# Other steps for the last layer's edges, scale, shift and final norms in a four-layer graph kernel

## The chip, the cores and the metric

The kernel runs on one core of one Trainium2 chip. The metric is the device time of one execution in microseconds; lower is better. Before the change, three runs gave 3883.53 to 3885.66 us, median 3884.97 us.

## The reference

There are 16 batches of 1024 nodes with 128 features, and one adjacency matrix for all. Three graph attention layers (8 heads of 16) come first, then one last layer of another kind. In short:

```python
# layers 0, 1, 2
scores = einsum('bnhd,bmhd->bhnm', h @ Wq, h @ Wk) / 4
attn = softmax(where(adj == 0, -inf, scores))
x = layer_norm(h + (attn @ (h @ Wv)) @ Wo + bo) * ln1_g + ln1_b
x = layer_norm(x + relu(x @ W1 + b1) @ W2 + b2) * ln2_g + ln2_b
# last layer
h = x @ W
e = leaky_relu((h @ a_src)[:, :, None] + (h @ a_dst)[:, None, :], 0.2)
att = softmax(where(adj == 0, -inf, e))
out = ln_gamma * layer_norm(att @ h + x) + ln_beta
```

Everything is in 32-bit floating point.

## The kernel before

**Blocks and steps.** A block is one batch through one of the three attention layers. There are 48 blocks, in passes of four batches: layer 0 of batches 0 to 3, layer 1 of the same four, layer 2 of the same four, then the next four batches (L848). A block has 32 steps: two head groups `g`, two halves of the queries `qh`, eight key tiles `kt`. Below, 11:29 means step 29 of block 11, counted from 0. In one step TensorE (PE) makes four score matmuls (L546). One half of the scores goes to ScalarE (ACT) for the exponential (L554) and then to GpSimd (POOL), which multiplies by the 0/1 mask (L555). The other half gets an additive mask on VectorE (DVE, L558) and then its exponential on ScalarE (L570). In ten of the 32 steps, listed in `BOTH_ON_DVE`, both halves take the second way and POOL has no product. The attention matmuls of a step (L575) run four steps later (`AHEAD`), into one PSUM accumulator.

**Other work between the steps.** All other work is cut into small tasks. `put` appends a chain of tasks, each with a gap in steps after the one before it and with flags. `piece` is called once per step. It takes at most one task that issues PE work per step; tasks with `*` in their flags come free beside it. A chain with a table (`AT`) has its tasks at fixed steps. `POOL_FREE` names the only steps at which tasks with `~` or `^` may be taken. `need` forces the tasks up to a mark at once; `need(source(m + 1))` does so at the head of a block, for the input of the next one.

- `proj_tasks` (L458) makes the queries and keys of the next block. Each half is split in a high part (ScalarE, L473) and a low part (VectorE, L474 or L478), and the copies in `stack` (L531) put them in place, 16 transfers at step 24 and 16 at step 1.
- `post_tasks` (L595) is the rest of a layer: output projection, norm, FFN, norm. `normalise` (L425) runs on POOL: negate the mean (L434), add epsilon (L435), power -0.5 (L436), subtract and scale per tile (L442). Its residual scale and shift (L633) are two POOL operations at steps 22 and 24.
- `last_tasks` (L702) is the last layer of one batch. It transposes x (L346), makes the node values (`nodes`, L721), sends eight rows twice as small copies to `g_rows` and `h_rows` (`send_rows`, L753, 16 transfers), and then, for each of eight tiles v, makes the edges (eight matmuls L773, and four masked maxima on VectorE, L778) and aggregates them two turns later (64 PE matmuls L384, then L798, L799 and the statistics on VectorE). Two POOL operations named `scaled` (L717, L718, both through L811) multiply x by ln2_g and add ln2_b; aggregates need their result. After four tiles `norm` normalises the lower half, after eight the upper; two POOL operations each (L811) apply gamma and beta, and `store` writes a half out in four transfers.

The last layers of a pass lie in the blocks of the next pass: batch 0's begins in block 10, batch 3's ends in block 16. Blocks 22 to 28 and 34 to 40 repeat this. The last pass's lies in blocks 46 and 47 and in a tail after the last step.

**What sets the order.** On PE, ScalarE and SyncE (SP) instructions stand in the order of the program. On VectorE and POOL a scheduler orders them by priority; `tc.issue_after` keeps an instruction behind another on its engine. `behind["pool"]` is the latest mask product, `low[n]` is the low part made at step n. One PSUM bank `t` serves all tasks, so a task's matmuls wait until the task before has been read out. SP issues nearly all transfers, in order; a transfer that waits holds back those behind it. There are five buffers for x, so the fetch of a later batch waits until the stores of an earlier one have landed.

Of the kernel before, what the change touches and what calls it, by code (L numbers as in the profile page):

```python
# [15 lines left out]
OP = mybir.AluOpType  # L16
AX = mybir.AxisListType

P = 128
# [4 lines left out]
SLOT = 32  # L24
# [5 lines left out]
LANES = 4  # L30
# [7 lines left out]
STACK_AT = 24  # L38
AT_END = {3: (12, 21, 22, 24, 25, 26, 27, 28, 30, 31), 2: (8, 9, 13, 14, 15, 16, 17, 18, 20, 21)}
AHEAD = 4  # L40
POOL_FREE = {"~": (0, 1, 2, 3, 4, 5, 6, 22, 23), "^": (30, 31, 0, 1, 2, 3, 4, 5, 6)}
BOTH_ON_DVE = (3, 7, 8, 15, 23, 24, 26, 28, 30, 31)
TILES = {"w": 8, "x": LANES + 1, "last": 2}
BLOCKED = -57344.0
# [76 lines left out]
def fast_path(ctx: ExitStack, tc: tile.TileContext, a: dict, out: bass.AP, flag):  # L121
    nc = tc.nc
    x_dram, adj = a["x"], a["adj"]
    B, N, D = x_dram.shape
    NT = N // P
# [14 lines left out]
    def bank():  # L140

        if head[0] or tail[0]:
            return slot()[:, :512]
        return psum.tile([P, 512], F32, tag="t", name="t", bufs=1)
# [14 lines left out]
    def tokens(v):  # L159

        return v.rearrange("(h j t e) d -> j e h t d", h=2, j=4, t=4)
# [33 lines left out]
    mask01 = const.tile([P, NT, N], F8W)  # L195
# [51 lines left out]
    wl = {}  # L247
# [177 lines left out]
    def normalise(n, ts):  # L425

        scalars(n, ts)
        subtract_scale(n, ts)

    def scalars(n, ts):  # L430

        mv = n[2]
        m, v = mv[:, ts, 0], mv[:, ts, 1]
        nc.gpsimd.tensor_scalar(m, m, -1.0, None, op0=OP.mult)  # L434
        nc.gpsimd.tensor_scalar(v, v, EPS, None, op0=OP.add)  # L435
        nc.gpsimd.tensor_tensor(v, v, half_neg[:, ts], OP.pow)  # L436

    def subtract_scale(n, ts):

        z, _, mv = n  # L440
        for t in range(ts.start, ts.stop):
            nc.gpsimd.tensor_scalar(z[:, t, :], z[:, t, :], mv[:, t, 0:1], mv[:, t, 1:2], op0=OP.add, op1=OP.mult)  # L442
# [79 lines left out]
    behind, low = {}, {}  # L522
# [179 lines left out]
    def last_tasks(b):  # L702
        s = {}
# [17 lines left out]
        def nodes(t0, t1):  # L721
            def run():
                col, ts = s["col"], slice(t0, t1)

                halves = [slice(max(t0, 4 * h), min(t1, 4 * h + 4)) for h in range(2)]
                halves = [(c, s["hd"][c.start // 4][:, c.start % 4:(c.stop - 1) % 4 + 1, :])
                          for c in halves if c.start < c.stop]
                ps = bank()
                for t in range(t0, t1):
                    by_columns(ps[:, (t - t0) * (D + 2):(t - t0 + 1) * (D + 2)],  # L730
                               s["xT", t // 4][:, t % 4 * P:(t % 4 + 1) * P], w_nodes)
                pv = ps[:, :(t1 - t0) * (D + 2)].rearrange("p (t d) -> p t d", d=D + 2)
                with soon():
                    nc.scalar.activation(col[:, 2, ts], pv[:, :, D + 1], AF.Exp, scale=NEG_SLOPE)
                    nc.scalar.activation(col[:, 0:2, ts].rearrange("p c t -> p t c"), pv[:, :, D:], AF.Exp,
                                         scale=1 - NEG_SLOPE)
                    for c, hd in halves:
                        nc.vector.tensor_mul(hd[:, :, :D], pv[:, c.start - t0:c.stop - t0, :D],
                                             col[:, 2, c, None].to_broadcast([P, c.stop - c.start, D]))
                for c, hd in halves:  # L740
                    nc.scalar.copy(hd[:, :, D], col[:, 2, c])
            return run
# [22 lines left out]
        def edges(v):  # L765
            def run():
                e = s["e", v] = edge_tile().rearrange("p (k q) -> p k q", q=P)
                half, t = slice(v // 4 * 512, v // 4 * 512 + 512), v % 4 * SLOT
                ps = slot()
                for k in range(4):  # L770
                    for r in range(2):
                        row = slice(64 * r + g0, 64 * r + g0 + 4)
                        nc.tensor.matmul(ps[:, r * 512 + k * P:r * 512 + (k + 1) * P], h_rows[row, k * P:(k + 1) * P],  # L773
                                         g_rows[row, half].rearrange("p (j q) -> p j q", j=4)[:, :, t:t + SLOT],
                                         start=True, stop=True)
                for j in range(4):
                    q = v // 4 * 512 + j * P + t
                    nc.vector.scalar_tensor_tensor(e[:, :, j * SLOT:(j + 1) * SLOT],  # L778
                                                   ps.rearrange("p (k q) -> p k q", q=P)[:, :, j * SLOT:(j + 1) * SLOT],
                                                   1.0, mask01[:, :, q:q + SLOT], op0=OP.max, op1=OP.mult)  # L780
            return run

        mul, add = nc.gpsimd.tensor_mul, nc.gpsimd.tensor_add
        late = b % LANES == LANES - 1 and b < B - 1

        def norm(h):
            def run():
                with tc.issue_after(behind["pool"]):
                    normalise(s["n"], slice(4 * h, 4 * h + 4))
            return run  # L790

        def aggregate(v):
            def run():
                need_if(("scaled", b))
                e, ps = s["e", v], bank()
                for t in range(NT):
                    by_columns(ps[:, :D + 1], e[:, t, :], s["hd"][t // 4][:, t % 4, :], start=(t == 0), stop=(t == NT - 1))
                nc.vector.reciprocal(s["col"][:, 3, v:v + 1], ps[:, D:D + 1])  # L798
                nc.vector.scalar_tensor_tensor(s["n"][0][:, v, :], ps[:, :D], s["col"][:, 3, v:v + 1],  # L799
                                               state["x", b][:, v, :], op0=OP.mult, op1=OP.add)  # L800
                stats(s["n"], slice(v, v + 1))
                if v % 4 == 3 and (v < NT - 1 or not late):
                    norm(v // 4)()
                if v == NT - 1:
                    check_range(s["col"].rearrange("p c t -> p (c t)"))
            return run

        def by_rows(op, z, v, n=NT):
            def run():
                with tc.issue_after(behind["pool"]):  # L810
                    op(z(), z(), rows(v(), n))  # L811
            return run
# [1 line left out]
        def x():  # L814
            return state["x", b]

        def y(h):
            return lambda: s["n"][0][:, 4 * h:4 * h + 4, :]

        def store(h):  # L820
            def run():
                y = s["n"][0]
                queue = nc.scalar if h and b == B - 1 else nc.sync
                for j in range(4):
                    queue.dma_start(tokens(out[b])[j][:, h], y[j * SLOT:(j + 1) * SLOT, 4 * h:4 * h + 4, :])

            return run

        def two(f, g):
            def run():  # L830
# [2 lines left out]
            return run  # L833

        tasks = [(5, xt(0), "+w +last +w +w"), (1, xt(1), "+w"), (2, nodes(0, 3), ""), (2, nodes(3, 6), ""),
                 (2, nodes(6, 8), "-w -w"), (2, rows_gh, ""), (1, send_rows, "*"), (7 if b < B - 1 else 4, edges(0), "")]
        for v in range(NT - 1):
            tasks.append((2, two(edges(v + 1), aggregate(v)), ""))
            if v in (4, 6):
                tasks.append((0, by_rows((mul, add)[v // 2 - 2], y(0), lambda v=v: wl[("ln_gamma", "ln_beta")[v // 2 - 2]], 4), "*"))  # L840
        up = "*^" if late else "*"
        tasks += [(2, aggregate(NT - 1), ""), (2, store(0), "-last -w -w *")] + [(0, norm(1), up)] * late
        tasks += [(1, by_rows(mul, y(1), lambda: wl["ln_gamma"], 4), up), (2 - late, by_rows(add, y(1), lambda: wl["ln_beta"], 4), up),
                  (3, store(1), "-x *")]
        return tasks


# [3 lines left out]
    now = [0]  # L851
# [3 lines left out]
    def put(tasks, mark, chain=None, first=False, table=None):  # L855

        if chain is None:
            chain = {"due": now[0], "queue": deque()}
            chains.insert(0 if first else len(chains), chain)
        for n, task in enumerate(tasks):  # L860
            at = now[0] // (4 * NT) * 4 * NT + (table or AT[mark[0]])[n] if mark[0] in AT else None
            chain["queue"].append(task + (mark if n == len(tasks) - 1 else None, at))
        return chain
# [16 lines left out]
    def is_due(chain):  # L880
        gap, tiles, at = chain["queue"][0][0], chain["queue"][0][2], chain["queue"][0][4]
        if now[0] >= 4 * NT * len(blocks):
            gap -= gap == 2
        for c in POOL_FREE:
            if c in tiles and not tail[0] and now[0] % (4 * NT) not in POOL_FREE[c]:
                return False
# [21 lines left out]
    with tc.manual_schedule(engines={mybir.EngineType.PE, mybir.EngineType.Activation, mybir.EngineType.DVE,  # L908
# [9 lines left out]
        ps = {}  # L918
# [55 lines left out]
    n = 0  # L974
    with tc.manual_schedule(engines={mybir.EngineType.PE, mybir.EngineType.Activation, mybir.EngineType.SP}):
        for m, (b, l) in enumerate(blocks):
# [3 lines left out]
            for at, (g, qh, kt) in enumerate((g, qh, kt) for g, qh in order for kt in range(NT)):  # L980
# [5 lines left out]
                if m + 1 < len(blocks):  # L986
# [5 lines left out]
                    if at == (6 if m == 0 else 0):  # L992
                        late = any(c["queue"][-1][3] == ("xP", m + 1) for c in chains)
# [6 lines left out]
                if FIRST <= n < FIRST + 4:  # L1000

                    with tc.manual_schedule(engines={mybir.EngineType.DVE}):
                        e = score_step(step)
                        neighbours(4 + n - FIRST)
                        masks(4 + n - FIRST, mask_rows(4 + n - FIRST))
                else:
                    e = score_step(step)
# [26 lines left out]
    ps = bank()  # L1034
# [226 lines left out]
```

## Time and profile before

| what | value |
|---|---|
| median of three runs | 3884.97 us |
| the profiled execution | 3886.72 us |
| its span, first to last instruction | 3884.9 us |
| PE busy | 3710.5 us (96%) |
| VectorE busy | 3460.0 us (89%) |
| POOL busy | 3477.8 us (90%) |
| ScalarE busy | 3295.4 us (85%) |
| mean granted PE clock | 0.987 |
| additive masks, L558 | 2016 of 1212 ns |
| mask products on POOL, L555 | 1056 of 2029 ns |
| edge maxima, L778 | 512 of 415 ns |
| pow on POOL, L436 | 179 of 1196 ns |
| subtract and scale on POOL, L442 | 896 of 448 ns |

The profile is one execution. All times within it are counted from the first instruction. Busy time of an engine includes no waiting; "idle before" names the wait just ahead of an instruction and the instruction or transfer that ended it. The granted clock is the share of TensorE's full speed that the hardware allowed in a stretch. The first score matmul of block 10 starts at 745.0 us, of block 11 at 817.7, 12 at 918.0, 13 at 1012.9, 14 at 1103.1, 15 at 1189.0. The last block's first is at 3669.2 and the tail begins at about 3770.

### The profile page before, as it was taken

To read this page: it belongs to the slowest core of one execution; us is meant where nothing else is said; L and a number is where in the kernel's file an instruction comes from. 1 tells how busy PE (TensorE), PEld (TensorE's weight loads), DVE (VectorE), ACT (ScalarE), POOL (GpSimd) and SP (SyncE) were. 2 spreads that over 40 slices of the span, in tenths; PEclk is the share of its full clock that TensorE was granted. 3 is DMA by queue.
4 is the path that set the end of the run, shared out by engine and by line. 5 is a ranking of instruction groups with operands and counts; after the bars stand their busy time and mean duration, and the time that the engine had idled before them with its cause. 6 is when DMAs were issued, how large, how long until landed. Compare 5 with 4: busy or idle time off the path is not lost.

```text
span 3884.9 us, 109698 instructions
## 1 busy us (share of the span) xinstructions
PE 3710.5 (96%) x44385; PEld 1513.9 (39%) x44385; DVE 3460.0 (89%) x5860; ACT 3295.4 (85%) x3797; POOL 3477.8 (90%) x2971
## 2 busy tenths in 40 slices
PE   7999999999999999999999999999999999999998
PEld 2333333344444333334444433333444433333346
DVE  6999999988989899998898999999889998999876
ACT  7989999977888999997788899999677799999860
POOL 4899999988988999998888999999788899999885
PEclk8999999999999999999999999999999999999998
DMA  5434324322233324332233324324222323423200
GB/s 138 114 74 101 96 72 107 90 67 67 73 79 84 103 69 104 91 80 74 67 85 79 93 67 101 96 72 101 70 70 63 96 72 90 107 69 104 71 5 24
DMA packets 245887, 319.28 MB, mean 82 GB/s; under 512 B 51072, under 2 KB 174208, under 8 KB 245376
## 3 DMA queue, kind: packets, MB, share of 16 engines
q1 hardware_dynamic: 243840, 311.52, 31.5%
q8 instruction: 353, 5.78, 0.6%
q14 instruction: 158, 1.29, 0.1%
q10 hardware_dynamic: 1536, 0.68, 0.1%
HBM read 58.53 MB, written 51.38 MB: 28 GB/s over the span
## 4 chain that ended last, share of the span: by engine, by line
POOL 45%; PE 38%; ACT 7%; DVE 5%; issue 3%; SPq 1%; DMA 1%; DVEq 0%; ACTq 0%; POOLq 0%
POOL e L555 27%; PE acc L575 13%; PE t L384 12%; PE s L546 9%; POOL x L442 6%; POOL x L633 4%; POOL mv L436 4%; ACT e L554 3%; ACT e L570 3%; DVE e L558 3%; PE s L773 2%; POOL x L811 1%; PE s L384 1%; POOL A L590 1%; POOL mv L435 1%
## 5 line engine op out<-in xcount | busy, mean ns | idle before, releaser
L558 DVE TENSOR_TENSOR e<-s,mask_add 128x1024 f32<-128x1024 f32 x2016 | 2377.8, 1212 | 203.7 <-PE s L546 175.5
L555 POOL TENSOR_TENSOR e<-e,mask 128x1024 f32<-128x1024 f32 x1056 | 2120.1, 2029 | 215.3 <-ACT e L554 201.9
L570 ACT ACTIVATE e<-e 128x1024 f32<-128x1024 f32 x2016 | 2109.9, 1062 | 175.9 <-DVE e L558 148.7
L575 PE MATMUL acc<-e,v 128*17 128x512 f32 x12288 | 1625.1, 601 | 70.3 <-POOL e L555 57.0
L554 ACT ACTIVATE e<-s 128x1024 f32<-128x1024 f32 x1056 | 1085.0, 1027 | 264.8 <-PE s L546 260.4
L546 PE MATMUL s<-Wq,Wk 64*128 64x512 f32 x6144 | 1195.1, 458 | 29.6 <-DVE e L558 17.0
L546 PEld LDWEIGHTS s<-Wq,Wk 64*128 64x128 f32 x6144 | 498.7, 185 | 1080.8 <-issue 386.9
L575 PEld LDWEIGHTS acc<-e,v 128*17 128x17 f32 x12288 | 204.7, 95 | 584.3 <-issue 350.2
L442 POOL TENSOR_SCALAR x<-x,mv 128x128 f32<-128x128 f32 x896 | 388.1, 448 | 19.4
L436 POOL TENSOR_TENSOR mv<-mv,half_neg 128x4 f32<-128x4 f32 (+1 forms) x179 | 214.1, 1196 | 14.0
L384 PE MATMUL t<-hd,ee 128*32 128x129 f32 x6720 | 214.9, 280 | 7.0 <-DVE lo L474 6.6
L414 DVE BATCH_NORM_STATS2 st<-x 128x6 f32<-128x128 f32 x896 | 204.4, 282 | 7.7
L384 PE MATMUL t<-x1T,W 128*32 128x512 f32 x1520 | 200.8, 600 | 1.4 <-DVE parts L750 1.3
L778 DVE SCALAR_TENSOR_TENSOR ee<-s,mask 128x256 f32<-128x256 f32 x512 | 180.2, 415 | 24.2 <-PE s L773 20.7
L384 PEld LDWEIGHTS t<-hd,ee 128*32 128x32 f32 x6720 | 187.1, 112 | 22.6 <-issue 11.2
L384 PEld LDWEIGHTS t<-W,hT 128*32 128x32 f32 x6080 | 171.0, 111 | 59.3 <-issue 48.7
L384 PE MATMUL t<-W,hT 128*32 128x128 f32 x6080 | 185.1, 274 | 0.1
L421 DVE TENSOR_TENSOR x<-t,x 128x512 f32<-128x512 f32 x191 | 129.1, 676 | 36.4 <-PE t L384 35.6
L590 POOL TENSOR_TENSOR A<-tt,recs 128x256 f32<-128x256 f32 x192 | 120.0, 625 | 43.5 <-DVE recs L589 43.5
L650 ACT ACTIVATE hT<-t,b 128x512 f32<-128x512 f32 x190 | 130.8, 688 | 13.6 <-PE t L384 12.7
L586 DVE STREAM_TRANSPOSE tt<-acc 128x512 f32<-128x512 f32 x192 | 135.5, 706 | 0.0
L358 DVE STREAM_TRANSPOSE xb<-x 128x512 f32<-128x512 f32 x164 | 115.1, 702 | 10.1 <-POOL x L442 9.8
(145 smaller groups left out, 2515.8 us busy)
## 6 DMA issues: line engine op xcount, KB each, us to landing
Wk<-hi SPq DMA_DIRECT2D x384, 128.0 KB
Wk<-lo SPq DMA_DIRECT2D x384, 128.0 KB
Wq<-hi SPq DMA_DIRECT2D x384, 128.0 KB
Wq<-lo SPq DMA_DIRECT2D x384, 128.0 KB
tr<-xb SPq DMA_DIRECT2D x656, 64.0 KB
x1T<-tr SPq DMA_DIRECT2D x90, 256.0 KB
xT<-tr SPq DMA_DIRECT2D x74, 256.0 KB
x<-in_x_dram SPq DMA_DIRECT2D x124, 64.0 KB
```

The source lines that it names most:

```text
L384: nc.tensor.matmul(dst[j:j + SLOT, :], cols, rhs, start=start, stop=stop)
L414: nc.vector.bn_stats(st[:, t, :], z[:, t, :])
L436: nc.gpsimd.tensor_tensor(v, v, half_neg[:, ts], OP.pow)
L442: nc.gpsimd.tensor_scalar(z[:, t, :], z[:, t, :], mv[:, t, 0:1], mv[:, t, 1:2], op0=OP.add, op1=OP.mult)
L546: nc.tensor.matmul(ps[:, r * 512:(r + 1) * 512], k[64 * r:64 * r + 64, kt * P:(kt + 1) * P], q[64 * r:64 * r + 64, q0:q0 + 512], start=Tru ...
L554: nc.scalar.activation(ev, psv, AF.Exp, scale=HD ** -0.5)
L555: behind["pool"] = nc.gpsimd.tensor_mul(ev, ev, m).ins
L558: behind["dve"] = nc.vector.tensor_add(ev, psv, m).ins
L570: nc.scalar.activation(ev, ev, AF.Exp, scale=HD ** -0.5)
L575: nc.tensor.matmul(acc[j * SLOT:j * SLOT + HD + 1, :], v_bufs[m % 2][:, kt, 2 * j + g, :], e[:, j, :], start=first, stop=last)
L590: nc.gpsimd.tensor_mul(state["A"][:, qh, :, g, :], tt[:, :, :HD], rec[:, :, None].to_broadcast([P, 16, HD]))
L778: nc.vector.scalar_tensor_tensor(e[:, :, j * SLOT:(j + 1) * SLOT], ps.rearrange("p (k q) -> p k q", q=P)[:, :, j * SLOT:(j + 1) * SLOT], 1 ...
```

## The change

There are four edits.

1. In the last layer, the gap before the first edges is 9 turns instead of 7 for every fourth batch (0, 4, 8, 12). For batch 15 it stays 4, for the others 7.
2. The steps at which the `scaled` operations may be taken are 0 to 6, 27, 28 and 29 instead of 0 to 6, 22 and 23.
3. The masked maxima of the edges are issued behind the low part of the step before, where there was one.
4. For batch 15, tiles 4 to 7 are each normalised, scaled, shifted and stored by themselves, as a chain of four tasks put at the head of the list when the tile is aggregated, instead of together after tile 7. The four transfers of such a store go to SP and ScalarE's queue in turns; before, the upper half's four went to ScalarE's queue. `norm`, `y` and `store` take a slice of tiles instead of a half.

```diff
-POOL_FREE = {"~": (0, 1, 2, 3, 4, 5, 6, 22, 23), "^": (30, 31, 0, 1, 2, 3, 4, 5, 6)}
+POOL_FREE = {"~": (0, 1, 2, 3, 4, 5, 6, 27, 28, 29), "^": (30, 31, 0, 1, 2, 3, 4, 5, 6)}
...
-                    nc.vector.scalar_tensor_tensor(e[:, :, j * SLOT:(j + 1) * SLOT],
-                                                   ps.rearrange("p (k q) -> p k q", q=P)[:, :, j * SLOT:(j + 1) * SLOT],
-                                                   1.0, mask01[:, :, q:q + SLOT], op0=OP.max, op1=OP.mult)
+                    with tc.issue_after(low[now[0] - 1]) if now[0] - 1 in low else nullcontext():
+                        nc.vector.scalar_tensor_tensor(e[:, :, j * SLOT:(j + 1) * SLOT],
+                                                       ps.rearrange("p (k q) -> p k q", q=P)[:, :, j * SLOT:(j + 1) * SLOT],
+                                                       1.0, mask01[:, :, q:q + SLOT], op0=OP.max, op1=OP.mult)
...
-                if v % 4 == 3 and (v < NT - 1 or not late):
-                    norm(v // 4)()
+                if b == B - 1 and v > 3:
+                    put([(0, norm(slice(v, v + 1)), "*"), (0, by_rows(mul, y(slice(v, v + 1)), lambda: wl["ln_gamma"], 1), "*"),
+                         (0, by_rows(add, y(slice(v, v + 1)), lambda: wl["ln_beta"], 1), "*"),
+                         (0, store(slice(v, v + 1)), "*")], ("out", v), first=True)
+                elif v % 4 == 3 and (v < NT - 1 or not late):
+                    norm(slice(v - 3, v + 1))()
...
-                queue = nc.scalar if h and b == B - 1 else nc.sync
                 for j in range(4):
-                    queue.dma_start(tokens(out[b])[j][:, h], y[j * SLOT:(j + 1) * SLOT, 4 * h:4 * h + 4, :])
+                    queue = nc.scalar if j % 2 and b == B - 1 and ts.start > 3 else nc.sync
+                    queue.dma_start(tokens(out[b])[j][:, ts.start // 4, ts.start % 4:(ts.stop - 1) % 4 + 1],
+                                    y[j * SLOT:(j + 1) * SLOT, ts, :])
...
-                 (2, nodes(6, 8), "-w -w"), (2, rows_gh, ""), (1, send_rows, "*"), (7 if b < B - 1 else 4, edges(0), "")]
+                 (2, nodes(6, 8), "-w -w"), (2, rows_gh, ""), (1, send_rows, "*"), (4 if b == B - 1 else 9 if b % LANES == 0 else 7, edges(0), "")]
...
-        tasks += [(1, by_rows(mul, y(1), lambda: wl["ln_gamma"], 4), up), (2 - late, by_rows(add, y(1), lambda: wl["ln_beta"], 4), up),
-                  (3, store(1), "-x *")]
+        if b < B - 1:
+            tasks += [(1, by_rows(mul, y(h1), lambda: wl["ln_gamma"], 4), up),
+                      (2 - late, by_rows(add, y(h1), lambda: wl["ln_beta"], 4), up), (3, store(h1), "-x *")]
```

More of the change, by code (lines that the diff above doesn't have):

```diff
@@ L784, in last_tasks, with norm @@
         late = b % LANES == LANES - 1 and b < B - 1
-        def norm(h):
+        def norm(ts):
             def run():
                 with tc.issue_after(behind["pool"]):
-                    normalise(s["n"], slice(4 * h, 4 * h + 4))
+                    normalise(s["n"], ts)
             return run
@@ L815, in x, with y, store @@
             return state["x", b]
-        def y(h):
-            return lambda: s["n"][0][:, 4 * h:4 * h + 4, :]
-        def store(h):
+        def y(ts):
+            return lambda: s["n"][0][:, ts, :]
+        def store(ts):
             def run():
                 y = s["n"][0]
-                queue = nc.scalar if h and b == B - 1 else nc.sync
                 for j in range(4):
-                    queue.dma_start(tokens(out[b])[j][:, h], y[j * SLOT:(j + 1) * SLOT, 4 * h:4 * h + 4, :])
+                    queue = nc.scalar if j % 2 and b == B - 1 and ts.start > 3 else nc.sync
+                    queue.dma_start(tokens(out[b])[j][:, ts.start // 4, ts.start % 4:(ts.stop - 1) % 4 + 1],
+                                    y[j * SLOT:(j + 1) * SLOT, ts, :])
             return run
@@ L839, in last_tasks @@
             if v in (4, 6):
-                tasks.append((0, by_rows((mul, add)[v // 2 - 2], y(0), lambda v=v: wl[("ln_gamma", "ln_beta")[v // 2 - 2]], 4), "*"))
+                tasks.append((0, by_rows((mul, add)[v // 2 - 2], y(slice(0, 4)), lambda v=v: wl[("ln_gamma", "ln_beta")[v // 2 - 2]], 4), "*"))
         up = "*^" if late else "*"
-        tasks += [(2, aggregate(NT - 1), ""), (2, store(0), "-last -w -w *")] + [(0, norm(1), up)] * late
-        tasks += [(1, by_rows(mul, y(1), lambda: wl["ln_gamma"], 4), up), (2 - late, by_rows(add, y(1), lambda: wl["ln_beta"], 4), up),
-                  (3, store(1), "-x *")]
+        h1 = slice(4, NT)
+        tasks += [(2, aggregate(NT - 1), ""), (2, store(slice(0, 4)), "-last -w -w *")] + [(0, norm(h1), up)] * late
+        if b < B - 1:
+            tasks += [(1, by_rows(mul, y(h1), lambda: wl["ln_gamma"], 4), up),
+                      (2 - late, by_rows(add, y(h1), lambda: wl["ln_beta"], 4), up), (3, store(h1), "-x *")]
         return tasks
```

## The prediction

> **What bounds the kernel now.** I read the page first: PE 96% busy, VectorE 89%, ScalarE 85%, POOL 90%. An average over stages says little, so I cut the span at the first score matmul of each block (32 steps of one batch and layer) and asked for busy times by stretch. Columns: stretch, its length, busy time and count of PE, weight loads, VectorE (DVE), ScalarE (ACT), POOL, then the granted PE clock.
>
> ```profile
> 463.00:533.40 70.40, 68.53 (x708) 24.09 (x704) 65.43 (x99) 67.06 (x75) 67.63 (x56) 1.00 0.35 91
> 817.70:918.00 100.30, 93.61 (x1357) 44.69 (x1353) 83.52 (x168) 70.48 (x88) 79.09 (x73) 0.97 0.26 68
> 918.00:1012.90 94.90, 92.16 (x1324) 44.75 (x1320) 82.52 (x164) 69.90 (x82) 79.21 (x73) 0.98 0.28 71
> ```
>
> A plain block (463) is PE at 97%. Blocks 11 and 12, which also carry the last layer of batches 0 and 1, hold 6.7 and 2.7 us of PE idle and a clock below 1. Block 13 has 0.5 us of idle. PE's work is the same after the change, so it can win only idle PE time and lost clock, and lose only by new PE waits. Next, PE's timeline for idle time over 1 us in blocks 10 to 13 (in brackets: idle before, releaser):
>
> ```profile
> 823.32 0.63 PE L773 MATMUL s<-g_rows,h_rows 4*128 4x128 f32 x7 [3.64 <-DMA h_rows<-parts]
> ...
> 909.56 1.91 PE L575 MATMUL acc<-e,v 128*17 128x512 f32 x8 [2.48 <-POOL e L555]
> ...
> 946.85 3.46 PE L384 MATMUL t<-hd,ee 128*32 128x129 f32 x60 [2.21 <-DVE lo L474]
> ```
>
> These are steps 11:0 (block:step), 11:29 and 12:10. The groups of batches 4 and 8 repeat them (3.66, 2.49, 2.21 and 4.68, 2.50, 2.20 us). Each is followed by 3.4 us at half clock:
>
> ```profile
> 909.30:912.70 3.40, 3.14 (x16) 0.55 (x16) 0.00 (x0) 0.13 (x1) 3.40 (x4) 0.51 0.02 5
> 1320.10:1323.50 3.40, 3.14 (x28) 0.76 (x28) 1.87 (x2) 1.70 (x3) 3.40 (x3) 1.00 0.36 92
> ```
>
> The second row follows an idle of 1.80 us and keeps clock 1.00. After 909.56 eight attention matmuls took 1.68 us against 0.87 elsewhere, and eight FFN matmuls 1.72 against 0.97: about 1.6 us lost per drop.
>
> [...] The rows show drops after 2.21 and 2.48 us, so 4.8. [...] I take the rows: drop from about 2.2 us, none up to 1.8.
>
> **Edges two turns later** (batches 0, 4, 8; batch 12's edges land on step 47:2 in both built orders). The last row copy is issued until 822.15 and PE resumes at 823.32. Moved to step 11:2, PE first does steps 11:1 and 11:2 (attention of 11:0 ends at 819.3; bare steps such as 12:0 to 12:2 take 1.65 us each): 819.3 + 3.3 = 822.6, so 0.7 us of waiting remains. Gain 2.9 + 1.6 = 4.5; third group 2.9 + 3.2 (its drop is 6.8 us long) = 6.1. All steps of batches 0 to 2 move two turns; SP's order of transfers is unchanged before the tail.
>
> **Scale and shift at 27 and 29** (POOL, 2.38 us each). POOL is full from 869.6 to 914, and at step 22 the scale stands between two residual operations:
>
> ```profile
> 900.46 2.40 POOL L633 TENSOR_TENSOR x<-x,ln_g 128x1024 f32<-128x1024 f32 x1
> 902.82 2.38 POOL L811 TENSOR_TENSOR x<-x,ln_g 128x1024 f32<-128x1024 f32 x1
> 905.17 2.38 POOL L633 TENSOR_TENSOR x<-x,b 128x1024 f32<-128x1024 f32 x1
> 907.50 3.96 POOL L555 TENSOR_TENSOR e<-e,mask 128x1024 f32<-128x1024 f32 x2
> ```
>
> Without it the multiplication of step 25 ends at 909.5 - 2.4 = 907.1; PE asks for it at 907.08 less 0.7 (a 0.43 us POOL wait at 11:24 goes, a 0.28 us transpose now comes later) = 906.4. Idle 0.7 to 0.9 instead of 2.48: gain 1.6 + 0.4 + 1.6 = 3.6. Block 10 has a 0.59 us POOL wait from the same place: gain 0.5. Behind the new places, step 29's product ends at 914.1 and is asked for at 12:1, about 917; covered.
>
> The new cost is step 12:29. There the built order queues five operations on POOL ahead of the product of 13:0: gamma half 1.29, shift 2.39, beta half 1.27, scale 2.40, shift 2.38, together 9.7 us. Summed from the multiplication of 12:27 (released about 1000.6): product to 1002.6, norm of batch 1's upper half 3.3, aggregate copy 0.6, product of 29 to 1008.5, the five to 1018.2, product of 13:0 to 1020.2. PE wants it at 13:4, 1022.5: covered by 2.3. But batch 1's upper store waits for beta at 1013.5 instead of 1006.5, and SP holds behind it the fetch of batch 6, 16 stack copies and 16 row copies: the rows end at 1035.7 + 7.2 = 1042.9, land 1.2 later at 1044.1; edges at 13:14 ask at 1045.7. Cover 1.6 us; I charge 0.4.
>
> **Masks behind the low half.** The only place where VectorE's order of these two changes is 12:10:
>
> ```profile
> 944.68 1.42 DVE L778 SCALAR_TENSOR_TENSOR ee<-s,mask 128x256 f32<-128x256 f32 x4
> 946.02 0.68 DVE L474 TENSOR_TENSOR lo<-t,hi 128x512 fp32r<-128x512 f32 x1
> ```
>
> The low half frees the one PSUM bank t that the aggregate at 946.85 needs. Ahead of the masks it ends at 945.3, PE starts at 945.4: idle 0.75, gain 1.45 + 1.6 = 3.05. The masks end at 946.7, needed two steps later; nothing else queues. If ScalarE's high half were late the masks would wait too, bound 0.7 us.
>
> **New waits at 14:0.** Two turns later, batch 2's last aggregate is forced at the head of block 14, straight behind FFN matmuls in the same bank: PE waits for VectorE's add, about 0.9 us, where a score step used to lie between. It ends near 1103.1 instead of 1099.8, one product (2.0) goes ahead of its norm, so beta ends 4.4 later, at 1112.7. Batch 7's fetch takes batch 2's buffer:
>
> ```profile
> 1111.63 4.60 SPq L168 DMA_DIRECT2D x<-in_x_dram  x8
> ```
>
> So 1116.0 to 1120.6, the seventh copy landed at about 1121.5 to 1122.2 (1.2 to 1.8 us landing, by the row copies and transposes); PE transposes it at 1120.95. Wait about 1.1, then 0.5 for the product of 14:5 at 14:9, less some of a 1.13 us VectorE wait at 14:10 that PE then no longer reaches early. Cost 2.0 a group, from 0.5 (all hidden) to 4.5 (one drop more).
>
> **Tail.** At 47:27 the scale (2.4) now stands ahead of the norm of the last batch's lower half, which PE waits for. The product of 27 comes 1.3 earlier, so the norm is 1.1 late: +1.1 (0 to 2.4). At the end four tiles are normalised singly:
>
> ```profile
> 3869.33 1.29 POOL L811 TENSOR_TENSOR x<-x,ln_beta 128x512 f32<-128x512 f32 x1
> ...
> 3872.84 1.04 POOL L436 TENSOR_TENSOR mv<-mv,half_neg 128x4 f32<-128x4 f32 x1
> 3873.99 1.74 POOL L442 TENSOR_SCALAR x<-x,mv 128x128 f32<-128x128 f32 x4
> 3875.81 1.26 POOL L811 TENSOR_TENSOR x<-x,ln_gamma 128x512 f32<-128x512 f32 x1
> ```
>
> No row shows a one-tile pow or scale. From two sizes each (pow 1.04 at 4 columns, 1.67 at 8; scale 1.27 at 512, 2.38 at 1024) I estimate 0.57 and 0.44. With starts: 0.30 + 0.31 + 0.68 + 3 x 0.52 = 2.85 us a tile. POOL is free at 3870.6, tiles come every 2.5 us, but POOL starts late, so all four queue: 3870.6 + 11.4 = 3881.9, against 3878.4. Bounds: pow 0.3 gives 10.3, pow 1.04 gives 13.3. The last store issues two copies per queue in place of four on ScalarE:
>
> ```profile
> 3878.44 2.44 ACTq L825 DMA_DIRECT2D out_dram<-x  x4
> ```
>
> That gives back 1.2, and smaller copies perhaps 0.3: +2.0 (0.5 to 4).
>
> **Sum.** A group: 4.5 + 3.6 + 0.5 + 3.05 - 0.4 - 2.0 = 9.25; the third 10.85; together 29.35; tail -3.1: -26.2 us. The profiled execution took 3886.7 (span 3884.9), so 3860.5 in its own terms; the median of the runs shown is 3885.0, so 3859.
>
> **The rivals.**
> All new waits stay hidden and the small ones too: 11.65 + 11.65 + 13.25 less 1 in the tail = -35.5, 3849. For it: PE stalls near each other overlap. Against: the bank at 14:0 has no cover. 20%.
> Half the gain comes: the shortened idles (0.7 to 0.9) still drop the clock, or POOL, full in block 11, keeps PE waiting there. Three drops of 1.6 in three groups, plus 1.6: 16 us back, 3875. Against: idles of 1.1 to 1.8 keep the clock, and POOL still sat idle 0.53 at 869.6. 16%.
> Slower: the store-behind-POOL chain at 12:29 and 14:0. If POOL is D us later than my sum, 13:14 waits D - 1.6 and 14:7 D + 1.1, each with a drop of 1.6. Three groups gain 36.5 in all, less the tail's 3.1 and 2.7 at the bank: 30.7 = 3 x (2D + 2.7) at D = 3.8. With D = 6, 3898. For it: two multiplications ahead of a norm are 4 us. Against: the built order has only the one I counted. 7%.
> No effect: D about 3.8, or gaps that return at the next step; 3885. 7%.
> The forecast, 3859, has 50%.
>
> The range 3848 to 3876 takes in the forecast, the first rival and most of the second. About 0.2% (7.8 us) is what a measurement of this kernel tells from no change. Faster 0.86, same 0.07, slower 0.07.
>
> **What would show it.** Right: PE idle before the first edge matmuls of 11:2, before 11:29's attention and before 12:10's aggregate each below 1 us, no half clock there; block 11 near 93 us, block 12 near 92; POOL's last operation near 3882 relative to today's end. Wrong: idle above 2 us at 13:14, at 14:0 or before the transposes of 14:7, or a half clock in block 14; a one-tile pow near 1 us; idle that reappears at 11:24 to 11:29.

## The result and the profile after

The changed kernel takes 3870.65 us, the median of six runs (3868.4 to 3875.15). The kernel before took 3885.66 us beside it (six runs, 3883.53 to 3889.17). The ratio is 0.996 with a 95% interval of 0.9949 to 0.9971: about 15 us faster where 26 were forecast. The profiled execution took 3870.8 us (span 3869.0), 15.9 less than the profiled one of before.

Blocks 11 to 14 of the first group come first, from the busy times by stretch of the changed kernel (columns as before: stretch, length, PE, weight loads, VectorE, ScalarE, POOL, then the granted clock):

```profile
817.73:911.93 94.20, 92.26 (x1358) 44.28 (x1354) 83.86 (x168) 70.26 (x88) 81.13 (x75) 0.98 0.30 72
911.93:1002.38 90.45, 89.76 (x1300) 42.97 (x1296) 81.99 (x162) 69.85 (x78) 76.35 (x72) 1.00 0.26 70
...
1094.86:1184.09 89.23, 84.22 (x1085) 36.73 (x1082) 76.83 (x136) 71.14 (x89) 80.56 (x68) 0.98 0.33 85
```

Block 11 fell from 100.3 to 94.2 us and block 12 from 94.9 to 90.45. Block 14, in the third row, grew from 85.9 to 89.2 and holds 5.0 us of PE idle. Block 13 grew from 90.2 to 92.5. The idle places are in PE's timeline of the changed kernel (idle before in brackets, with its releaser); the last row is that of the kernel before at 14:10:

```profile
824.03 0.63 PE L773 MATMUL s<-g_rows,h_rows 4*128 4x128 f32 x7 [1.01 <-DMA h_rows<-parts]
...
936.53 1.98 PE L384 MATMUL t<-hd,ee 128*32 128x129 f32 x64 [0.54 <-DVE lo L474]
...
1113.76 0.63 PE L346 MATMUL t<-identf,x 128*128 128x128 f32 x4 [0.99 <-DVE e L558]
1118.20 1.05 PE L575 MATMUL acc<-e,v 128*17 128x512 f32 x8 [0.92 <-POOL e L555]
1124.51 0.65 PE L384 MATMUL t<-w_nodes,xT 128*32 128x130 f32 x16 [2.75 <-DVE lo L474]
```

```profile
1129.54 0.65 PE L384 MATMUL t<-w_nodes,xT 128*32 128x130 f32 x16 [1.13 <-DVE lo L474]
```

The first row is 11:2. It waits 1.01 us where 3.64 stood at 11:0, and PE needs 0.63 us for seven small matmuls there as it did before. The second row is 12:10, 0.54 for 2.21. At 11:29 no idle is left; 0.77 us came at 11:31. The last three rows of the changed kernel are new or larger: 14:7, 14:9 and 14:10, which was 1.13.

All idle of blocks 10 to 14 that is over 0.3 us, and the half-clock windows of 3.4 us that start there (the idles of 0.42 us that both kernels have are left out):

| group | idle before | idle after | windows before | windows after | sum of block lengths, after less before |
|---|---|---|---|---|---|
| batches 0 to 3 | 12.4 us | 8.6 us | 3 | 2 | -5.64 us |
| batches 4 to 7 | 12.3 us | 8.5 us | 3 | 2 | -5.53 us |
| batches 8 to 11 | 13.9 us | 11.5 us | 4 | 1 | -6.39 us |

At 1.6 us lost in a window, the estimate that the prediction worked out from the trace, the first row gives -3.8 - 1.6 = -5.4 us. The third sums to -2.4 - 4.8 = -7.2, which is 0.8 too much.

### The profile page after: what moved, and what is told of

Its sections match the earlier page's. It is cut to its first block, busy times and chain, and to the rows that moved or that the text cites. A ratio compares the mean times of both kernels' runs of the same rounds, so it can differ in the third digit from the quotient of the medians.

```text
span 3869.0 us, 109722 instructions
## 1 busy us (share of the span) xinstructions
PE 3703.0 (96%) x44385; PEld 1509.2 (39%) x44385; DVE 3461.7 (89%) x5860; ACT 3294.0 (85%) x3797; POOL 3483.2 (90%) x2986
## 4 chain that ended last, share of the span: by engine, by line
POOL 41%; PE 40%; ACT 6%; DVE 5%; issue 3%; SPq 3%; DMA 1%; DVEq 0%; ACTq 0%; POOLq 0%
POOL e L555 25%; PE acc L575 14%; PE t L384 13%; PE s L546 10%; POOL x L442 6%; POOL mv L436 3%; POOL x L633 3%; ACT e L554 3%; DVE e L558 3%; ACT e L570 2%; PE s L773 2%; SPq L531 1%; POOL x L816 1%; POOL A L590 1%; PE s L384 1%
## 5 line engine op out<-in xcount | busy, mean ns | idle before, releaser
L436 POOL TENSOR_TENSOR mv<-mv,half_neg 128x4 f32<-128x4 f32 (+2 forms) x182 | 215.3, 1183 | 14.6
```

## The experiments

**Each edit alone.** Four kernels, each the one before with one of the four edits. The first has gap 9, the second the new steps for scale and shift, the third the masks behind the low half, the fourth the new ending. The diffs are those parts of the change.

Edges alone:

> The kernel before with one edit: the first edges of every fourth batch have gap 9 instead of 7. Theory: this edit gains at 11:2 only its idle (3.64 to about 1.0 us, so 2.6 us a group, the half-clock window staying), and it is this edit, by pushing the last-layer chain and its store two steps back, that makes blocks 13 and 14 longer; then blocks 11 to 14 together change by -2 to +2 us a group and the whole by -5 to +5 us, about 3884. Rival: the longer blocks 13 and 14 come from the scale/shift steps or from the mask order; then edges alone give -2.6 us a group, about 3877.

Scale and shift alone:

> The kernel before with one edit: scale and shift of the last layer may be taken at steps 0 to 6 and 27 to 29 instead of 0 to 6, 22 and 23. Theory: the 2.48 us idle at 11:29 and its half-clock window go (3.3 to 3.6 us a group), 47:30 costs 1.1 us, blocks 13 and 14 keep their length: -9 us, about 3876. Rival: the two instructions, now later on POOL, push the following POOL work and the store back and blocks 13 and 14 grow by about 4 us a group as in the changed kernel: about 3886.

Masks alone:

> The kernel before with one edit: the edge masks of a step are issued behind the low half of the step ahead. Theory: the 2.21 us idle at 12:10 falls to about 0.55 us and its half-clock window goes, 3.1 to 3.4 us a group: -9 to -10 us, about 3875.5. Rival: at 12:10 only the idle is gained and the clock window comes elsewhere: -5 us, about 3880.

Ending alone:

> The kernel before with one edit: the last four tiles of the last batch are normalised and stored one by one. Theory: POOL ends 3 to 3.5 us later (four times 2.85 us instead of one chain over four tiles), the last stores land 1.2 to 1.6 us sooner after it: +1.5 to +2.5 us if the half-clock time of the tail is as before, about 3887.5; with 3.4 us less of half clock, as in the changed kernel's profile, about 0: 3885.5. Rival (the edit does what its form suggests): the stores of the first tiles overlap the work of the later ones and the end comes sooner, -2 to -4 us: about 3882.

| kernel | median, runs | ratio to before (95%) | blocks 10 to 14, us by group |
|---|---|---|---|
| before, beside them | 3887.06, 48 | | |
| edges | 3881.81, 21 | 0.9988 (0.9982 to 0.9995) | -1.6, -0.1, -2.5 |
| scale and shift | 3879.65, 12 | 0.9983 (0.9974 to 0.9992) | -1.8, -2.3, -3.0 |
| masks | 3879.07, 13 | 0.9981 (0.9973 to 0.9989) | -3.2, -1.4, -2.6 |
| ending | 3889.13, 13 | 1.0005 (0.9997 to 1.0014) | +0.7, +0.1, +0.2 |

Within their intervals the ratios add up: 0.12 + 0.17 + 0.19 - 0.05 = 0.43% against 0.40% for the whole change. The blocks say where each edit works.

With edges alone, block 13 is longer by 2.3 and block 14 by 2.8 us in all three groups. With the other edits alone neither changes by more than 0.1. So this edit carries the whole loss of blocks 13 and 14. The half-clock window that was expected to stay at 11:2 went in all three groups, behind waits of 0.42, 0.56 and 1.81 us. (About 0.8 us of block 13 is a piece of projection that only moved over the border. In the kernel below that leaves it where it was, block 12 is 1.3 us longer, and 0.45 of that is an idle at 12:5.)

Scale and shift alone gain 0.6 in block 10, but block 11 wins only 0.9 to 2.2. PE's timeline of this kernel at 11:0 shows why:

```profile
823.32 1.08 PE L773 MATMUL s<-g_rows,h_rows 4*128 4x128 f32 x7 [4.33 <-DMA h_rows<-parts]
```

PE resumes at the same time as before (823.32). The row copies on SP's queue set it, not PE. The 0.68 us won in block 10 became waiting: 4.33 for 3.64. Seven matmuls take 1.08 instead of 0.63 us because they now fall in a half-clock stretch, which grew from one window to two. In the kernel before they take 1.08 us as well at 2722.84, in a stretch of two windows at half clock (6.83 us from 2721.81).

The masks gave 3.1 to 3.2 us in block 12, as expected, in every group. The 1.55 us that group 2 lost again lies in block 23, where a second half-clock window came. The ending alone can't be told from no change; in its profile the last score starts 114.87 us before the end, and 114.94 in the kernel before.

**What the clock follows.** These kernels hold the same idle with and without a drop. In the kernel with edges alone, PE waits 2.20 us at 12:10 and again 2.20 us at 24:10. Busy times by stretch of that kernel, cut at its clock records, the window with the idle and the one behind it, for 12:10 and then for 24:10:

```profile
937.13:940.54 3.41, 1.71 (x64) 1.74 (x64) 1.55 (x4) 0.36 (x1) 1.92 (x1) 1.00 0.04 13
940.54:943.95 3.41, 3.41 (x39) 1.04 (x32) 2.95 (x7) 2.54 (x4) 1.49 (x1) 1.00 0.00 0
1882.66:1886.07 3.41, 1.21 (x20) 0.58 (x13) 2.99 (x6) 2.04 (x3) 3.41 (x2) 1.00 0.20 56
1886.07:1889.48 3.41, 3.41 (x64) 3.18 (x64) 0.00 (x0) 0.00 (x0) 0.21 (x1) 0.50 0.02 5
```

The first idle left PE busy for 1.71 of a window's 3.41 us, because part of it fell into the window before; the clock stayed 1.00. The second lay whole in one window, which left 1.21; the next ran at 0.50. In each trace the half-clock records start on one grid of 3.413 us. In the kernel before, those at 223.25, 824.00, 909.33 and 946.88 us lie 61, 237, 262 and 273 times that behind the first, at 15.04, and each of the four is 3.41 us long. I counted PE's busy share in every such window of all thirteen profiled executions, from 30 us after the first score to the last one, where the clock was full:

| PE's busy share of the window | next window at half clock | at full clock |
|---|---|---|
| under 46.5% | 55 | 0 |
| 46.5 to 55% | 18 | 17 |
| 55 to 71% | 21 | 207 |
| over 71% | 0 | 13654 |

In the traces of before and after alone, windows taken where the next one ends by the last score too, the rows hold 13 and 0, 2 and 1, 5 and 34, 0 and 2095. In the thirteen, the 55 windows in which PE was idle for more than 1.83 of 3.413 us were all followed by 3.4 us at half clock, and of the 13654 with less than 1.0 us idle none was. Between the two, this share alone does not decide. The borders were chosen on these same windows: they sort what was counted here, and no run shows that they hold elsewhere.

What filled a window seems to matter too. At 11:2 of the changed kernel the share was 70%, and half clock followed:

```profile
821.38:824.80 3.42, 2.41 (x22) 1.13 (x22) 1.87 (x3) 3.42 (x4) 3.42 (x3) 1.00 0.09 17
824.80:828.21 3.41, 3.41 (x32) 1.33 (x34) 3.41 (x6) 1.12 (x2) 1.92 (x1) 0.51 0.54 151
```

Of the 2.41 us, about 0.9 were edge matmuls (L773), whose operands have 4 partitions, where those of the scores have 64 and those of the attention 128. In the third row of the table, half clock followed 15 of the 29 windows that hold edge matmuls, and 6 of the 199 that hold none; these 6 all lie near 200 us, with the two-column matmuls of L286 in them. Counted without L773 and L286, no window over 52% was followed by half clock, and 78 of the 79 under 46.5% were. So these small matmuls seem to count for little, and if so, waiting for the edges costs clock for the edges' own time as well. This is read from the counts; no run isolates it.

**The third batch's edges back, then the second's.** Is it the late end of the third batch's chain that costs blocks 13 and 14? Two kernels, each the changed one with one of these lines:

```diff
-(4 if b == B - 1 else 9 if b % LANES == 0 else 7, edges(0), "")
+(4 if b == B - 1 else (9, 7, 5, 7)[b % LANES], edges(0), "")
+(4 if b == B - 1 else (9, 5, 7, 7)[b % LANES], edges(0), "")
```

> The changed kernel with gap 5 instead of 7 for the first edges of the third batch of each group, which puts them back to 13:12 and the end of that batch's chain back to 13:30 and 14:0; nothing before block 13 moves. Theory: the losses of blocks 13 and 14 come from the late end of this chain (bank at 13:31, then its second half's scale and shift, store and fetch, which hold the stack of block 14 on SP's queue). The idles at 13:15, 13:31, 14:7 and 14:9 go and 14:10 falls back to 1.13 us: 4.2 us a group, 12.6 in all: ratio to before 0.9928. Rival: the losses come from the second batch, two turns late in block 12 (its store and fetch at 13:0), and stay: ratio 0.996.

> The changed kernel with gap 5 for the first edges of the second batch of each group: its chain is back at its old steps from 12:4 on, and the third batch's with it. Theory: as with the third batch alone, and 0.37 us at 13:7 as well: 4.6 us a group, 13.7 in all, ratio 0.9925. Rival: the old steps of block 12 bring back its idles (0.44 at 12:5, up to 2.2 at 12:10): 1 to 2 us a group lost again, ratio 0.9935 to 0.994.

With the third batch's gap at 5, the median is 3875.92 us (6 runs), ratio 0.997 (0.9958 to 0.9981) beside a kernel before of 3887.48: no faster than the change itself. The theory was right on block 14: 13:15, 13:31, 14:7 and 14:9 are empty and 14:10 is back at 1.14, 1.13 and 1.12 us. But I had moved the edges and not the row copies ahead of them, which still leave at 13:7. PE's timeline of this kernel at 13:12:

```profile
1031.83 0.63 PE L773 MATMUL s<-g_rows,h_rows 4*128 4x128 f32 x7 [2.73 <-DMA h_rows<-parts]
```

A new wait of 2.73, 2.78 and 3.73 us, each with a half-clock stretch behind it, took back what block 14 gave. It is the wait of 11:0 over again. The tail was longer too, 120.3 us from the last score to the end against 114.5, with 41.8 us of it at half clock against 25.7.

With the second batch's gap at 5, its whole chain is back at the old steps, and the third's row copies with it. All of blocks 13 and 14's loss is gone (14:10 at 1.13), blocks 10 to 14 are 10.5 to 12.5 us shorter than before in each group, and the last score ends 31.6 us sooner. Yet the median is 3868.79 us (5 runs), ratio 0.9954 (0.9942 to 0.9967). Some 10 us of that went in the tail, 124.7 us from the last score to the end against 114.5. PE's timeline there:

```profile
3791.05 0.30 PE L773 MATMUL s<-g_rows,h_rows 4*128 4x128 f32 x1 [1.05 <-DMA g_rows<-parts]
3796.70 1.08 PE L773 MATMUL s<-g_rows,h_rows 4*128 4x128 f32 x7 [5.35 <-DMA h_rows<-parts]
```

In the last group the same gap put batch 13's edges ahead of batch 14's first transposes. Batch 14's row copies were issued from 46.3 to 57.2 us after the last score, in the changed kernel from 41.5 to 52.5. Its edges waited 6.4 us for them, where the changed kernel waits 0.33 at that place. Half clock held for 35.9 us of this tail, against 25.7.

**The stack copies on ScalarE's queue.** At 14:10 the change's PE waits for the low half, and that for the high half. ScalarE's timeline and SP's, both of the changed kernel:

```profile
1123.00 0.59 ACT L473 CAST hi<-t 128x512 fp32r<-128x512 f32 x1 [3.48 <-DMA Wk<-hi]
```

```profile
1104.98 2.23 SPq L830 DMA_DIRECT2D out_dram<-x  x4
1108.71 3.65 SPq L168 DMA_DIRECT2D x<-in_x_dram  x8
1112.46 0.48 SPq L531 DMA_DIRECT2D Wk<-hi  x1
...
1120.20 0.61 SPq L531 DMA_DIRECT2D Wk<-hi  x1
```

The split for block 15 may overwrite the high-half tile only when the copies that stack block 14's second half have read it. These stand on SP behind store and fetch, the last K copies of the high half were issued at 1120.20, and ScalarE wrote at 1123.00. To test it I let ScalarE issue those 16 copies:

```diff
-behind["stack"] = nc.sync.dma_start(
+behind["stack"] = (nc.scalar if g and m > 12 and m % 12 == 2 else nc.sync).dma_start(
```

> The changed kernel with the 16 transfers that stack the second half of K and Q for block 14 (and 26, 38) issued by ACT instead of SP, so that they no longer queue behind store and fetch. Theory: the wait at 14:10 is a write after read (the next block's split overwrites the hi and lo tiles that these transfers still read); they now end some 10 us sooner and 14:10 falls from 2.75, 1.17 and 1.89 us to 1.13; the idles at 13:31, 14:7 and 14:9 stay; ACT pays 16 issues: -2.4 us by the idles, up to -4 with the half-clock window that follows in group 1: ratio 0.995 to 0.9955. Rival: 14:10 waits for POOL or for the fetch, stays as it is, and the issues cost ACT about 1 us a group: ratio 0.996 to 0.997.

It took 3917.8 us (5 runs), ratio 1.0078 (1.0065 to 1.0091): 47 us over the changed kernel. ScalarE's timeline of this kernel:

```profile
1096.60 0.57 ACTq L531 DMA_DIRECT2D Wk<-hi  x1
...
1107.28 3.61 ACTq L531 DMA_DIRECT2D Wq<-lo  x2
...
1116.17 1.02 ACT L554 ACTIVATE e<-s 128x1024 f32<-128x1024 f32 x1 [18.79 <-DMA Wq<-hi]
```

Sixteen issues of about 0.6 us each, and the waits that some of them carry (before the fifth ScalarE issued nothing from 1099.1 to 1105.8), held ScalarE's exponentials for 18.8 us. PE waited 17 us at 14:3, 26:3 and 38:3. 14:10 did fall to 1.14, but behind such a stall everything had caught up, so it tells the two readings of 14:10 apart no better than the trace did. One more copy of the high and low tiles would test it directly; this wasn't tried.

**Mending it.** Three kernels more and an earlier one. The first has gap 5 for the second batch only in the groups ahead of the last. The second has this and the old ending and the old scale/shift steps in the last block. The third, beside that, has gaps 10 and 4 for the first and second batch. The earlier one has the old ending with the third batch at gap 5.

```diff
+(4 if b == B - 1 else (9, 5, 7, 7)[b % LANES] if b < B - LANES else 9 if b == B - LANES else 7, edges(0), "")
...
+(4 if b == B - 1 else (10, 4, 7, 7)[b % LANES] if b < B - LANES else 7, edges(0), "")
```

The old steps in the last block come from this, in the planner's test of what is due:

```diff
+            if c == "~" and now[0] // (4 * NT) == len(blocks) - 1 and now[0] % (4 * NT) in (22, 23):
+                continue
             if c in tiles and not tail[0] and now[0] % (4 * NT) not in POOL_FREE[c]:
```

> The changed kernel with gap 5 for the first edges of the second batch in the first three groups only; the last group as in the changed kernel. Theory: with gap 5 in all four groups the last score ended 31.6 us sooner than before, but the tail took 124.7 instead of 114.5 us, because the thirteenth batch's edges at the first steps of the tail changed the order there; without that the 5 us a group of blocks 13 and 14 reach the end: ratio to before 0.992 to 0.9925. Rival: the tail is longer for another reason (how the clock windows fall, or a late transfer of h_rows that varies from run to run), and the ratio stays at 0.995.

> As the last one, but with the old ending and the old scale/shift steps in the last block. Theory (sums of single runs): 1.1 us less at 47:30 and 1.9 us less for the ending: 3 us under the last one, ratio 0.9915. Rival: with the tail's times scattering by several us from how the windows fall, no difference: 0.992 to 0.9925.

> As the last one, but in the first three groups the first batch's edges start at gap 10 (11:4 instead of 11:2) and the second's at gap 4, which keeps that batch at 12:4. Theory: the wait for h_rows at 11:2 (1.0, 1.2 and 2.9 us in the changed kernel) and the half-clock windows that follow it go; 11:4 waits for nothing: 5 to 8 us less, ratio 0.990. Rival: two turns later the first batch's last aggregate meets the next batch's transposes at 11:20 to 11:22, and 1 to 2 us a group come back there: ratio 0.9915.

> The kernel before with the edges of the first batch two turns later but the third batch's gap 5, with the new scale/shift steps except in the last block, with the new mask order, and with the old ending. Theory (the sum of what the single runs showed): the 12.6 us of the third batch, 1.1 at 47:30 and 1.9 of the ending, 15.6 us under the changed kernel: ratio 0.992, about 31 us under before. Rival: the ending's form is worth its price and the old one loses it: ratio 0.993.

| kernel | median, runs (range) | ratio to before (95%) |
|---|---|---|
| second batch at 5, first three groups | 3857.58, 5 (3856.06 to 3861.09) | 0.9925 (0.9912 to 0.9939) |
| and the old ending | 3856.89, 5 (3854.54 to 3857.09) | 0.992 (0.9906 to 0.9933) |
| and gaps 10 and 4 | 3851.9, 4 (3851.55 to 3854.01) | 0.9908 (0.9893 to 0.9923) |
| third batch at 5, old ending | 3878.27, 12 (3870.48 to 3885.75) | 0.9978 (0.997 to 0.9987) |

The first row is as the theory had it. Blocks 13 and 14 are within 0.2 us of before in each group, the last score ends 30.8 us sooner and the tail takes 116.2. So the second batch's later edges had cost the change about 13 us (3870.65 less 3857.58, on different chips). In the profiles, blocks 13 and 14 got back 15.8 us in the three groups together, while blocks 11 and 12 gave up 1.5. The second row was to gain 3 us more and shows 0.7 between medians, which the intervals don't tell from nothing. One half of it was laid out wrongly: with the old steps allowed beside the new, the shift was taken at 47:27, ahead of the norm that PE waits for, and 47:30 grew from 2.23 to 3.55 us instead of falling to 1.2. So 1.3 us were lost there, and 1.9 were expected of the ending. In the profiled executions the tail was 4.5 us shorter, with 11.3 us less of it at half clock, and the last score 2.8 us later; how much of this is the ending is open. Gaps 10 and 4 took the wait at 11:2 away, in all three groups, for a new one of 0.9 us at 11:10, and in this kernel no half clock is left between 205 and 3635 us. The 5.0 us between medians are the low end of what was expected. Its runs and those of the row above don't overlap, though the two intervals do. The last row repeats the miss at 13:12 (2.47, 2.15 and 3.40 us); its runs spread over 15 us, and the profiled one is the fastest of the twelve.

## Why the prediction was right and where not

The sign was right, and so were the waits that it took away at 11:2, 11:29 and 12:10 and the price of POOL's operations in the tail. The size was off by 10 us: 3870.65 lies nearer to the rival of half the gain (3875) than to the forecast (3859), and the range held because it took in that rival. Most of the miss is in the clock; the rest is in the waits at 11:2 and in block 14.

- **Clock, the larger miss.** The sum took 4.8 us a group from half clock that goes, by "drop from about 2.2 us, none up to 1.8". Measured: 3, 3 and 4 windows before, 2, 2 and 1 after, so 3.2, 3.2 and 1.6 us a group less than forecast. That is 8 of the 10 us. At 11:2 a wait of 1.01 us was followed by a drop at 824.8, and the waits of block 14 drew two more. In the kernel with edges alone 0.42, 0.56 and even 1.81 us at this place drew none. A threshold on the single idle was the wrong form: 1.01 us here drew a drop and 2.20 us at 12:10 of the kernel with edges alone drew none. What sorts these runs better is PE's busy share of a window of the grid: 1.21 of 3.41 us ahead of a drop at 24:10 of that kernel, 1.71 without one at 12:10. At 11:2 the share was 2.41 of 3.42, and the edge matmuls in it seem to count for little. The row that stood for "none up to 1.8" could not show a threshold, since its idle, from 1318.24 to 1320.04, lies across the border of two windows at 1318.93 and left PE busy for 79 and 60% of them. The rival that kept these drops was priced at 16 us, of which half came.
- **Edges at 11:2.** PE came at 823.0 and the rows at 824.0, where the sum had 822.6 and 823.3. PE's side was 0.4 off. The rows' side was 0.7 late, because SP's chain ahead of them doesn't follow PE: their last issue ended at 822.86 against 822.15, though block 11 began at the same 817.7. The 0.5 us for block 10 was therefore no gain of its own, being ahead of a wait that SP sets; the kernel with scale and shift alone shows it, 4.33 for 3.64. In the third group the wait was 2.92 where 1.8 was left by the sum.
- **Scale and shift at 11:29.** Right that the 2.48 us go. The 0.7 to 0.9 us of POOL wait that was to stay did not come. The 0.77 at 11:31 only looks like it: it ends with VectorE's `parts`, and the kernel with edges alone, which leaves scale and shift where they were, has it too (the first row is of the changed kernel, the second of that one):

```profile
910.04 1.96 PE L384 MATMUL t<-W,hT 128*32 128x128 f32 x64 [0.77 <-DVE parts L750]
```

```profile
910.68 1.96 PE L384 MATMUL t<-W,hT 128*32 128x128 f32 x64 [0.77 <-DVE parts L750]
```

With scale and shift alone, 0.44 us for `parts` stands at 11:29 in the first group. So 0.77 is a cost of the edges that the sum had at nothing, and the agreement of the numbers is luck.
- **Masks at 12:10.** Right: 0.54 where 0.75 was forecast, no drop, 3.1 to 3.2 us a group alone for 3.05.
- **12:29 and 13:14.** POOL's queue held; edges at 13:14 waited for nothing. In its place came 0.37 at 13:7 and 0.44 at 13:15, together 0.81 at other places for 0.4 forecast.
- **The bank at 14:0.** Right: 0.81 for 0.9, met at 13:31's end.
- **Block 14.** The fetch was right in time: 1108.71, which is 1117.0 when block 14 is laid on the old one, for 1116.0. The wait at 14:7 was 0.99, 1.77 and 1.21 for 1.1. The profile names the fetch as its end only in the third group (`[1.21 <-DMA x<-in_x_dram]` at 3003.81); in the first it names a VectorE instruction, so the fetch is inferred there. The product's wait at 14:9 was 0.92, none and 0.72 for 0.5. The step that failed is "less some of a 1.13 us VectorE wait at 14:10". The wait grew to 2.75, 1.17 and 1.89. I had followed store and fetch on SP and not the 16 stack copies queued behind them, nor what their late end holds: the tile that block 15's split overwrites. That cause is read from the wait of 3.48 us in ScalarE's row and from 14:10's return to 1.13 wherever the chain ends sooner; no run isolates it.
- **Tail.** The 47:30 wait went from 1.21 to 2.27 as summed (+1.1). One-tile operations cost what was estimated, as POOL's timeline of the changed kernel shows:

```profile
3861.41 0.23 POOL L434 TENSOR_SCALAR mv<-mv 128x1 f32<-128x1 f32 x1
...
3862.00 0.57 POOL L436 TENSOR_TENSOR mv<-mv,half_neg 128x1 f32<-128x1 f32 x1
3862.68 0.45 POOL L442 TENSOR_SCALAR x<-x,mv 128x128 f32<-128x128 f32 x1
...
3863.74 0.45 POOL L816 TENSOR_TENSOR x<-x,ln_beta 128x128 f32<-128x128 f32 x1
```

A pow of one column took 0.57 for 0.57 estimated, a scale 0.45 for 0.44, a tile 2.87 for 2.85. The four tiles took 11.45 us from where POOL came free (3852.74 to 3864.19), for 11.4. Still the +2.0 us for the end is not in this profile (114.45 us from the last score, 114.94 before), because POOL came free 2.6 us sooner after the last score (98.1 for 100.7): 10.2 us of the tail's work ahead of it ran at half clock where 13.7 did before. The ending alone, over 13 runs, reads +1.9 us with an interval of -1 to +5. The 0.3 us that the sum gave to smaller copies is shown by no run.

So the groups gave 17.6 us for 29.35, block 47 cost 1.1, the stretch after the last score gave 0.5, and 1.1 us went elsewhere, where single windows at 200.2 and 1316.4 came and others went.

## What to carry to other kernels

A step that is moved later drags along every chain that is laid out behind it. Follow it to its last store, and on that queue to whatever stands behind the store, and ask which buffer that still reads. Moving the consumer of a transfer helps only as far as the transfer doesn't move, and a gain ahead of a wait that another queue ends is no gain. Where a trace shows half clock, count PE's busy share on the grid of the clock records ahead of it, as here: 55 of 55 windows under 46.5% were followed by it, none of 13654 over 71%. Look at what fills the windows between (55 to 71%: 15 of 29 with edge matmuls, 6 of 199 without), and keep a price on idles of 1 us as well, since 1.01 us was followed by a drop at 11:2. A number that agrees can come from another place: look at the releaser.

## What the runs showed of the hardware

In the traces of these thirteen kernels half clock began on a grid of 3.413 us. Counted by PE's busy share of the window just ended, it followed 55 of 55 windows under 46.5%, 18 of 35 between 46.5 and 55%, 21 of 228 between 55 and 71%, and none of 13654 over 71%. Of the 228, it followed 15 of 29 with edge matmuls (4 partitions) and 6 of 199 without. With edges alone, the same code with the same 2.20 us idle ran at 1.00 in one group (12:10) and at 0.50 in another (24:10). A copy of K issued from ScalarE took 0.55 to 0.61 us of its queue's time, one issued from SP 0.48 to 0.61. With 16 such transfers on ScalarE's queue, two copies of Q took 3.61 us together at 1107.28, nothing was issued from 1099.1 to 1105.8, and ScalarE's exponentials stood still for 18.8 us.
